# A graph layer with a segment maximum: the first sixteen gather steps of part one read stored B rows in place of x rows

## The chip, the core and the metric

The kernel runs on one core of one Trainium2 chip, in one launch. The metric is the device time of an execution in microseconds (us), stated as the median of several executions. In the tables below TensorE is called PE (its weight loads PEld), VectorE DVE, ScalarE ACT, GpSimd POOL, and the engine whose queue issues most of the transfers SP.

## The reference

The inputs are x (6250 nodes by 256 features), 100000 edges as two integer lists src and dst, sorted by dst, and two 256x256 weights with biases.

```python
x_src = x[src]
x_dst = x[dst]
theta_x = (x_dst - x_src) @ theta_w.T + theta_b
phi_x = x_src @ phi_w.T + phi_b
e = relu(theta_x + phi_x)
out = segment_max(e, dst, num_segments=6250)      # 0 for a node without edges
x = layernorm(x + out)
```

A message is x_dst @ theta + x_src @ (phi - theta) + bias. The first and the last term are the same for all edges of one node, so the maximum is needed only over B = x @ (phi - theta), at the rows that src names. The kernel computes B once for all nodes, takes maxima of rows of B by node, and adds the rest at the end.

## The kernel before, in words

**Preparation.** B is made in 13 shares of up to four tiles of 128 nodes. For each pair of tiles, PE transposes x (L779), ACT copies the result out of PSUM (L782), PE multiplies with the weights (L794), ACT copies B out (L797), and a transfer stores four tiles as rows of the DRAM tensor `b_rows` (L818). Meanwhile DVE finds where the second part's edges begin, fetches a window of 872 edges per partition (`dst_w`, `src_w`, L521), and builds a table of words from it (`fill_table`, L1005 and L1008, ten rounds).

**Part one** covers the nodes that stand first. Its edges lie as 81 steps of 128 edges. In each step one indirect transfer on POOL's queue gathers 128 rows (L528), and DVE runs a capped maximum along the steps (L699: one instruction for each step but the first). Eight steps make a group, a tile `g` of a ring of five; a finished group is stored to `maxima_1` (L714). Groups 0 and 1, which are sixteen steps, gather rows of x, because `b_rows` isn't there yet; `x_group` multiplies these rows by the weights in place, in pairs of steps, with the same four instructions as above. Groups 2 to 10 gather rows of `b_rows`. The end of part one's chain goes through PE (`tails_1`, transposes in L912).

**Part two** covers the other 44 tiles of nodes. For each of 17 slots of 383 rows of B, DVE picks which row each node wants in that slot (`choice`, L1037 to L1057, two slots at a time); `wanted` transposes the picks on PE (L1064) and stores them as `chosen_rows`; ACT and at times DVE turn them into one-hot matrices `hot` (L1121, L1123, L1126); PE multiplies the slot's rows, split into two terms (L1094 on ACT, L1095 on DVE), with them (L1134); and the maximum goes into `acc` (L1144 for slot 0, L1146 on DVE after that). What the slots leave over is written as a list (`list_pieces`, thirteen rounds on DVE, stored in L1289), fetched back by POOL in three transfers (L521), and run as 257 further steps of gather and maximum. At the end the sums are normalised and written.

**What sets the order.** Each engine works through its own instructions in order. A scheduler lays the order down when the program is built, from the order of the code and its own guesses of durations. Transfers on POOL's queue are tied to each other by `in_turn`, and L699 is tied to the gather of its step. Slot 0's L1095 stands behind `choice` of slots 8 and 9 (`ahead_of_run`). The driver at the end of the function calls `fill_table`, then `choice` and `wanted` in nine rounds, with one chunk of slot 0 after the fifth, then two more chunks, then `run_1` for groups 0 and 1, and then the rest of part one in turn with chunks and list pieces.

Of the kernel before, what the change touches and what calls it, by code (L numbers as in the profile page):

```python
# [54 lines left out]
STEPS = 8  # L55
# [1 line left out]
EARLY_SHARES = 10  # L57
RING = 5
FIRST_STEPS = 81
X_GROUPS = 2  # L60
TILES = 44
LIST = 257
WINDOW = 872
# [9 lines left out]
TABLE_BITS = 10  # L73
SLOT_BITS = 9
P_BITS = 7
EARLY_STEPS = 6
TERMS_BEHIND = 4
ROWS_AT = 2
TERMS_AT = 4
# [356 lines left out]
def gnn_kernel(ctx: ExitStack, tc: tile.TileContext, x, src, dst, theta_w, theta_b, phi_w, phi_b, out):  # L436
# [30 lines left out]
    b_rows = dram.tile([N, D], FP, name="b_rows")  # L467
# [26 lines left out]
    def present(t, part, j0, n):  # L494
        return t[: LEFT1 if (part, j0, n) == LAST else P, :n, :]
# [31 lines left out]
    def gather(to, table, offsets, wait_for=None):  # L527
        one = nc.gpsimd.indirect_dma_start(  # L528
            out=to, out_offset=None, in_=table, in_offset=bass.IndirectOffsetOnAxis(ap=offsets, axis=0)
        )  # L530
# [19 lines left out]
    src_1 = const.tile([P, T1], I32, name="src_1")  # L550
    nc.sync.dma_start(src_1, flat(src, 0, [[T1, P], [1, T1]]))
    gathered = body.enter_context(tc.tile_pool(name="gathered", bufs=RING))
    groups = [(t0, min(STEPS, T1 - t0)) for t0 in range(0, T1, STEPS)]
    of_x = range(X_GROUPS)
    ring_tiles = {}

    def gather_group(i, table, a=0, b=STEPS):
        t0, n = groups[i]
        if i not in ring_tiles:
            ring_tiles[i] = gathered.tile([P, STEPS, D], FP, name="g")  # L560
        return [
            gather(ring_tiles[i][:, k, :], table, src_1[:, t0 + k : t0 + k + 1], hold(k)) for k in range(a, min(b, n))
        ]

    first_node = const.tile([P, 1], FP, name="first_node")
# [18 lines left out]
    in_turn(iota(starts, TILES, N1 - 1 + TILES, 0))  # L584
    in_turn(iota(first_node, 0, N1, TILES))
    in_turn(iota(ids[:, T + 1 :], 0, 0, T))
    gather_group(of_x[0], x, 0, EARLY_STEPS)


    dst_1 = search.tile([P, T1 + 2], I32, name="dst_1")  # L590
    dst_i = search.tile([P, T + 2], I32, name="dst_i")
# [71 lines left out]
        windows_fetched[0] = latest[0]  # L663

    search_edges()
    gather_group(of_x[0], x, EARLY_STEPS)

    ids_1 = const.tile([P, T1 + 3], FP, name="ids_1")
    one = nc.vector.tensor_copy(ids_1[:, : T1 + 2], dst_1)
    behind_in_order(one, window_found[0], "search ahead of the first part")  # L670
    early.close()
    for i in of_x[1:]:
        gather_group(i, x)

    iota(ids_1[:, T1 + 2 :], 0, 0, T1)
    start, chunk, after = ids_1[:, T1 + 2 :], ids_1[:, 1 : T1 + 1], ids_1[:, T1 + 1 : T1 + 2]
# [50 lines left out]
    with (  # L727
# [57 lines left out]
        def b_of(to, rows, kept=None):  # L785

            n = rows.shape[1]
            x_t = x_transposed(rows)
            if kept is not None:
                nc.sync.dma_start(kept, x_t[:, :n].rearrange("p h k n -> p (h k n)"))  # L790
            ps = ps_b.tile([P, 2, D], FP, name="ps_b")
            for h in range(n):
                for k in range(KC):
                    nc.tensor.matmul(  # L794
                        ps[:, h, :], x_t[:, h, k, :], weights[:, k, 0, :], start=(k == 0), stop=(k == KC - 1)
                    )
            nc.scalar.copy(to, ps[:, :n, :])  # L797

        def x_group(i):
            for q in range(0, STEPS, 2):  # L800
                rows = ring_tiles[i][:, q : q + 2, :]
                b_of(rows, rows)

        for number, share in enumerate(shares(4)):
            if number == X_AHEAD:
                bias_and_pads()
            n = share[2]
# [8 lines left out]
                kept = x_columns[:, at : at + w * KC * P] if share[0] == 2 else None  # L816
                b_of(b_sb[:, i : i + w, :], x_q[:, i : i + w, :], kept)
            nc.scalar.dma_start(node_rows(b_rows, *share), present(b_sb, *share))  # L818
        for i in of_x:
            x_group(i)  # L820

    acc_pool = body.enter_context(tc.tile_pool(name="accs", bufs=1))
    acc = acc_pool.tile([P, KC, OWN], FP, name="acc")
# [647 lines left out]


    parts = [(s, c) for s in range(NS) for c in range(len(CHUNKS))]
    groups_1 = list(range(X_GROUPS, len(groups)))
    todo = list(range(NT1))
    searched = [None]

# [17 lines left out]
    def next_group_1(n):  # L1495
        if groups_1:
            i = groups_1.pop(0)
            if held[0]:
                g_last, (t0, n_last) = ring_tiles[i - 1], groups[i - 1]
                for k in range(0, STEPS, 2):  # L1500
                    run_steps(1, g_last, range(k, k + 2), caps_1, t0)
                    gather_group(i, b_rows, k, k + 2)
                    if k % 4 == 2 and n > k // 4:
                        fetch_parts(1)
                nc.sync.dma_start(maxima_1t[:, t0 : t0 + STEPS, :], g_last)
            else:
                gathers = gather_group(i, b_rows)
                if i > X_GROUPS:
                    run_1(i - 1, gathers)
                fetch_parts(n)  # L1510
        if searched[0] is not None:
            next(searched[0])
            searched[0] = None
        if todo:
# [12 lines left out]
    for _ in range(2):  # L1527
        next_group_1(0)
    chunk_heads()
# [127 lines left out]
```

## Time and profile before

| what | value |
|---|---|
| time, median of 3 runs | 729.33 us (724.2 to 729.99) |
| profiled execution, its own time | 723.1 us |
| span of its trace | 721.3 us |
| PE busy | 653.8 us, 91% |
| DVE busy | 634.1 us, 88% |
| ACT busy | 510.1 us, 71% |
| POOL busy | 526.9 us, 73% |

The busy shares are means over stages with different limits, so they tell little of one place. The change touches the first 230 us or so; what counts is which engine is never idle there, and which wait ends last.

### The profile page before, as it was taken

The page shows a single profiled execution, that of the slowest core. Times are in us where ns is not written, and L with a number is a line of the kernel's source. Part 1 is how long each engine was busy: PE and PEld are TensorE (multiplying, and loading weights), DVE is VectorE, ACT ScalarE, POOL GpSimd, SP SyncE. Part 2 cuts the span into 40 slices and gives each one's busy share as a digit, 9 for nine tenths or more (in the row PEclk, how much of TensorE's full clock was granted, in tenths as well). Part 3 has the DMA queues.
Part 4 walks back from the last instruction along what each step waited for, and adds up shares of the span by engine and source line. Part 5 has one row for each costly group of instructions (what it writes and reads, how often), then busy time and mean ns, then how long its engine had stood idle before and what let it go on. Part 6 is the DMA issues. An engine that isn't in the chain of part 4 may idle for free.

```text
span 721.3 us, 9888 instructions
## 1 busy us (share of the span) xinstructions
PE 653.8 (91%) x2908; PEld 532.9 (74%) x2908; DVE 634.1 (88%) x1202; ACT 510.1 (71%) x597; POOL 526.9 (73%) x730
## 2 busy tenths in 40 slices
PE   4799977769798999999999999999999999969990
PEld 3688766657576888888888888888888888848870
DVE  6999999999997788989889788988988989898876
ACT  1344759679695876868778687977868778642676
POOL 6700277888815857888888888888888888848880
PEclk9999989799999999999999999999999999999996
DMA  8898563655656647777786977887776767655865
GB/s 257 296 352 300 178 205 95 225 194 171 190 197 201 208 153 224 242 228 256 221 277 213 335 263 245 273 291 256 222 248 219 250 203 247 207 188 181 293 242 214
DMA packets 60879, 167.06 MB, mean 232 GB/s; under 512 B 11896, under 2 KB 21905, under 8 KB 54673
## 3 DMA queue, kind: packets, MB, share of 16 engines
q1 hardware_dynamic: 39717, 107.15, 42.5%
q0 software_dynamic: 18976, 52.35, 24.7%
q10 hardware_dynamic: 2124, 6.84, 2.5%
q8 instruction: 25, 0.41, 0.2%
q14 instruction: 37, 0.30, 0.1%
HBM read 102.94 MB, written 63.36 MB: 231 GB/s over the span
## 4 chain that ended last, share of the span: by engine, by line
PE 62%; DVE 17%; POOL 6%; DMA 5%; ACT 5%; issue 4%; ACTq 0%; DVEq 0%; POOLq 0%
PE ps_f L1134 60%; POOL g L528 4%; DVE g L699 3%; DVE words L1008 2%; ACT hot L1123 1%; ACT hot L1126 1%; DVE work L1005 1%; POOL pause L498 1%; ACT x_f L1434 1%; DVE wide L1041 1%; DMA g<-maxima,place 1%; DMA dst_w<-in_dst_dram,window 1%; DMA dst<-in_dst_dram 1%; DMA dst_w<-list_words,run_start 1%; DMA list_words<-work 1%
## 5 line engine op out<-in xcount | busy, mean ns | idle before, releaser
L1134 PE MATMUL ps_f<-hot,terms 128*128 128x512 f32 x2156 | 512.0, 399 | 23.3 <-ACT hot L1126 9.9
L1134 PEld LDWEIGHTS ps_f<-hot,terms 128*128 128x128 f32 x2156 | 409.6, 192 | 120.2 <-ACT hot L1126 17.0
L528 POOL DMA_INDIRECT g<-b_rows,list_src x256 | 258.0, 1008 | 58.5 <-issue 35.1
L1123 ACT ACTIVATE hot<-want,minus_row 128x1024 fp32r<-128x1024 f16 x210 | 216.4, 1078 | 100.9 <-PE ps_f L1134 100.9
L1146 DVE TENSOR_TENSOR acc<-acc,ps_f 128x1024 f32<-128x1024 f32 x192 | 215.7, 1129 | 52.2 <-PE ps_f L1134 51.3
L1126 ACT ACTIVATE hot<-hot 128x2048 fp32r<-128x2048 f32 (+2 forms) x102 | 186.6, 1829 | 2.6
L699 DVE SCALAR_TENSOR_TENSOR g<-g,caps 128x256 f32<-128x256 f32 x335 | 160.7, 480 | 1.9
L528 POOL DMA_INDIRECT g<-b_rows,src x65 | 92.1, 1418 | 69.6 <-DMA b_rows<-b_sb 49.8
L498 POOL IOTA pause<- 128x160 f32 x312 | 97.3, 312 | 2.3
L794 PE MATMUL ps_b<-weights,x_t 128*128 128x256 f32 x260 | 62.1, 394 | 7.5 <-ACT x_t L782 7.1
L1121 DVE TENSOR_SCALAR hot<-want,row_id 128x1024 fp32r<-128x1024 f16 x84 | 61.6, 734 | 0.3 <-issue 0.3
L794 PEld LDWEIGHTS ps_b<-weights,x_t 128*128 128x128 f32 x260 | 49.2, 195 | 16.0 <-ACT x_t L782 9.8
L528 POOL DMA_INDIRECT g<-maxima,place x44 | 42.6, 968 | 17.8 <-DMA maxima<-g 10.9
L1389 PE MATMUL ps_e<-weights,kept 128*128 128x256 f32 x176 | 41.6, 379 | 0.0
L1419 ACT ACTIVATE squares<-x_f,r 128x256 bf16<-128x256 f32 x49 | 24.2, 494 | 21.9 <-DVE r L1416 21.9
L1389 PEld LDWEIGHTS ps_e<-weights,kept 128*128 128x128 f32 x176 | 33.5, 190 | 4.3
L797 ACT COPY b_sb<-ps_b 128x512 f32<-128x512 f32 (+1 forms) x25 | 14.4, 577 | 30.8 <-PE ps_b L794 21.8
L1434 ACT ACTIVATE x_f<-x_f,r 128x256 f32<-128x256 f32 x41 | 21.3, 587 | 5.7 <-DVE r L1426 5.7
L782 ACT COPY x_t<-ps_xt 128x512 f32<-128x512 f32 (+1 forms) x33 | 18.2, 589 | 7.9 <-PE ps_xt L779 7.6
L1399 DVE TENSOR_TENSOR g<-g,ps_e 128x512 f32<-128x512 f32 x22 | 15.1, 687 | 8.6 <-DMA g<-maxima,place 4.7
L528 POOL DMA_INDIRECT g<-in_x_dram,src x16 | 17.9, 1116 | 5.4 <-issue 4.1
L1144 ACT COPY acc<-ps_f 128x1024 f32<-128x1024 f32 (+1 forms) x12 | 11.3, 941 | 14.6 <-PE ps_f L1134 14.6
(251 smaller groups left out, 416.1 us busy)
## 6 DMA issues: line engine op xcount, KB each, us to landing
maxima<-g SPq DMA_DIRECT2D x42, 1024.0 KB
want<-chosen_rows SPq DMA_DIRECT2D x85, 256.0 KB
x_q<-in_x_dram SPq DMA_DIRECT2D x12, 512.0 KB
b_rows<-b_sb ACTq DMA_DIRECT2D x12, 512.0 KB
x_columns<-x_t SPq DMA_DIRECT2D x22, 256.0 KB
kept<-x_columns SPq DMA_DIRECT2D x11, 512.0 KB
raw<-b_rows SPq DMA_DIRECT2D x16, 256.0 KB
g<-b_rows,list_src POOLq DMA_INDIRECT x256, 4.3
```

What stands on the lines that cost most here:

```text
L498: return nc.gpsimd.iota(t, pattern=[[step, t.shape[1]]], base=base, channel_multiplier=per_partition, allow_small_or_imprecise_dtypes=True,)
L528: one = nc.gpsimd.indirect_dma_start(out=to, out_offset=None, in_=table, in_offset=bass.IndirectOffsetOnAxis(ap=offsets, axis=0))
L699: one = nc.vector.scalar_tensor_tensor(g[:, k, :], last[part], caps[:, t : t + 1], g[:, k, :], op0=ALU.min, op1=ALU.max)
L794: nc.tensor.matmul(ps[:, h, :], x_t[:, h, k, :], weights[:, k, 0, :], start=(k == 0), stop=(k == KC - 1))
L1121: nc.vector.tensor_scalar(hot[:, b, :], want, row_id[:, b : b + 1], None, op0=ALU.is_equal)
L1123: nc.scalar.activation(hot[:, b, :], want, AF.Abs, bias=minus_row[:, b : b + 1], scale=1.0)
L1126: nc.scalar.activation(apart, apart.bitcast(FP), AF.Relu, bias=1.0, scale=-1.0)
L1134: one = nc.tensor.matmul(ps[:, w : w + 512], terms[:, part, b, h * P : (h + 1) * P], hot[:, b, w : w + 512], start=(i == 0), stop=(i == n ...
L1146: one = nc.vector.tensor_tensor(to, to, ps, op=ALU.max)
L1389: nc.tensor.matmul(a[:, i, :], x_t[:, 2 * i + c, :], weights[:, c, 1, :], start=False, stop=(i == w - 1 and c == KC - 1))
L1419: nc.scalar.activation(squares, x_f[:, k, :], AF.Square, bias=mean[:, k : k + 1], scale=1.0, accum_out=var[:, k : k + 1])
L1434: nc.scalar.activation(x_f[:, k, :], x_f[:, k, :], AF.Identity, bias=mean[:, k : k + 1], scale=inv[:, k : k + 1])
```

## The change

Groups 0 and 1 no longer gather rows of x. The six gathers at the begin, the ten after the edge window, and `x_group` go away. After `fill_table` in the code, both groups are gathered from `b_rows` like all others, and their two `run_1` calls are tied to these gathers. The number of gathers (81), of bytes that they move, and of maxima on DVE stays as it was. The constant `X_GROUPS` is renamed `FIRST_GROUPS`, and `EARLY_STEPS` is dropped.

```diff
-    of_x = range(X_GROUPS)
     ring_tiles = {}
 
-    def gather_group(i, table, a=0, b=STEPS):
+    def gather_group(i, a=0, b=STEPS):
         t0, n = groups[i]
         if i not in ring_tiles:
             ring_tiles[i] = gathered.tile([P, STEPS, D], FP, name="g")
         return [
-            gather(ring_tiles[i][:, k, :], table, src_1[:, t0 + k : t0 + k + 1], hold(k)) for k in range(a, min(b, n))
+            gather(ring_tiles[i][:, k, :], b_rows, src_1[:, t0 + k : t0 + k + 1], hold(k)) for k in range(a, min(b, n))
         ]
...
     in_turn(iota(ids[:, T + 1 :], 0, 0, T))
-    gather_group(of_x[0], x, 0, EARLY_STEPS)
...
     search_edges()
-    gather_group(of_x[0], x, EARLY_STEPS)
-
...
     early.close()
-    for i in of_x[1:]:
-        gather_group(i, x)
...
-        def x_group(i):
-            for q in range(0, STEPS, 2):
-                rows = ring_tiles[i][:, q : q + 2, :]
-                b_of(rows, rows)
-
...
             nc.scalar.dma_start(node_rows(b_rows, *share), present(b_sb, *share))
-        for i in of_x:
-            x_group(i)
...
-                gathers = gather_group(i, b_rows)
-                if i > X_GROUPS:
+                gathers = gather_group(i)
+                if i > FIRST_GROUPS:
                     run_1(i - 1, gathers)
...
     fill_table()
+    first_gathers = [gather_group(i) for i in range(FIRST_GROUPS)]
     for s0 in range(0, NS, BATCH_S):
...
     fetch_parts(2)
-    for i in of_x:
-        run_1(i)
+    for i in range(FIRST_GROUPS):
+        run_1(i, first_gathers[i])
```

The changed kernel's lines lie up to 15 lower than the same lines before. POOL, from the edge window on, before (`dst_w` and `src_w` are the window, `g` a group of part one, `pause` a filler):

```order
L521 DMA dst_w<-in_dst_dram,window 128x872
L498 IOTA pause 128x160
L521 DMA src_w<-in_src_dram,window 128x872
L498 IOTA pause 128x160
L528 DMA g<-in_x_dram,src_72 128x256 x10
L498 IOTA order 128x1584
L498 IOTA chunk_1248 128x1
L1284 IOTA owner 128x1
L498 IOTA chunk_2064 128x1
L528 DMA g<-b_rows,src_72 128x256 x24
L498 IOTA wide 128x290
L528 DMA g<-b_rows,src_72 128x256 x41
```

and of the change:

```order
L520 DMA dst_w<-in_dst_dram,window 128x872
L497 IOTA pause 128x160
L520 DMA src_w<-in_src_dram,window 128x872
L497 IOTA pause 128x160
L497 IOTA order 128x1584
L497 IOTA chunk_1144 128x1
L1269 IOTA owner 128x1
L497 IOTA chunk_1960 128x1
L527 DMA g<-b_rows,src_72 128x256 x40
L497 IOTA wide 128x290
L527 DMA g<-b_rows,src_72 128x256 x41
```

Ten gathers from x are gone here and six more near the program's begin; 40 gathers from `b_rows` stand where 24 stood.

PE, at the end of B, before (`ps_b` is B, `ps` with `chosen` are the picks of two slots, `ps_f` the slots' products; `x_q` is a tile of x, `g` a group):

```order
L1064 MATMUL ps<-ident,chosen 88x128 x2
L794 MATMUL ps_b<-weights,x_t 128x256 x12
L779 MATMUL ps_xt<-ident,g 128x128 x10
L794 MATMUL ps_b<-weights,x_t 128x256 x8
L779 MATMUL ps_xt<-ident,g 128x128 x10
L1064 MATMUL ps<-ident,chosen 88x128 x2
L794 MATMUL ps_b<-weights,x_t 128x256 x12
L779 MATMUL ps_xt<-ident,g 128x128 x4
L1064 MATMUL ps<-ident,chosen 88x128
L794 MATMUL ps_b<-weights,x_t 128x256 x4
L1064 MATMUL ps<-ident,chosen 88x128
L1134 MATMUL ps_f<-hot,terms 128x512 x26
```

and of the change:

```order
L1049 MATMUL ps<-ident,chosen 88x128 x2
L786 MATMUL ps_b<-weights,x_t 128x256 x4
L1049 MATMUL ps<-ident,chosen 88x128
L1119 MATMUL ps_f<-hot,terms 128x512 x4
L1049 MATMUL ps<-ident,chosen 88x128
L1119 MATMUL ps_f<-hot,terms 128x512 x2
L1049 MATMUL ps<-ident,chosen 88x128
L1119 MATMUL ps_f<-hot,terms 128x512 x20
```

The 32 transposes of `g` and their 32 products are gone, and the first six slot products stand between the picks; the next twenty follow the fifth round of picks.

DVE, in the fourth round of `choice` (L1037 to L1057), before:

```order
L1041 TENSOR_TENSOR wide<-wide 128x1056
L699 TENSOR_SCALAR g<-g,caps_171 128x256
L1041 TENSOR_TENSOR wide<-wide 128x2x264
L699 TENSOR_SCALAR g<-g,caps_171 128x256
L1041 TENSOR_TENSOR wide<-wide 128x2x132
L1041 TENSOR_TENSOR wide<-wide 128x2x44
L699 TENSOR_SCALAR g<-g,caps_171 128x256
L1041 TENSOR_TENSOR wide<-wide 128x2x44
L699 TENSOR_SCALAR g<-g,caps_171 128x256
L1048 TENSOR_SCALAR at<-wide 128x88
L1049 COPY chosen<-at 128x88
L1053 TENSOR_TENSOR wide<-wide,at 128x2112
```

and of the change, from that round's L1048 on (now L1033) to the first minimum of the fifth round:

```order
L1033 TENSOR_SCALAR at<-wide 128x88
L691 TENSOR_SCALAR g<-g,caps_153 128x256
L1034 COPY chosen<-at 128x88
L1038 TENSOR_TENSOR wide<-wide,at 128x2112
L691 TENSOR_SCALAR g<-g,caps_153 128x256
L1042 TENSOR_TENSOR unused<-unused,wide 128x1056
L691 TENSOR_SCALAR g<-g,caps_153 128x256
L1042 TENSOR_TENSOR unused<-unused,wide 128x1056
L1022 TENSOR_SCALAR wide<-padded 128x1056 x2
L691 TENSOR_SCALAR g<-g,caps_153 128x256
L1026 TENSOR_TENSOR wide<-wide 128x1056
L691 TENSOR_SCALAR g<-g,caps_153 128x256
```

Group 0's seven maxima (L699, now L691) began inside the third round and ended in the fourth; now the first two stand just ahead of the rows shown, around the fourth round's last 44-wide minimum, and the seventh stands inside the fifth round, ahead of four of its minima. Each of them waits for its own gather. The seven are still all ahead of slot 0's L1095. Behind the first rounds of the list the order on every engine is as before.

More of the change, by code (lines that the diff above doesn't have):

```diff
@@ L59 @@
 FIRST_STEPS = 81
-X_GROUPS = 2
+FIRST_GROUPS = 2
 TILES = 44
@@ L75 @@
 P_BITS = 7
-EARLY_STEPS = 6
 TERMS_BEHIND = 4
@@ L1473, in gnn_kernel @@
     parts = [(s, c) for s in range(NS) for c in range(len(CHUNKS))]
-    groups_1 = list(range(X_GROUPS, len(groups)))
+    groups_1 = list(range(FIRST_GROUPS, len(groups)))
     todo = list(range(NT1))
@@ L1501, in next_group_1 @@
                     run_steps(1, g_last, range(k, k + 2), caps_1, t0)
-                    gather_group(i, b_rows, k, k + 2)
+                    gather_group(i, k, k + 2)
                     if k % 4 == 2 and n > k // 4:
```

## The prediction

> **What bounds the kernel now.** The change moves work in the first 230 us, so I read the stretches of that time first, then DVE's waits in them, then the single rows around the place. The busy time of each engine by stretch (columns: window, its length, then PE, PEld, DVE, ACT and POOL busy with counts, granted PE clock, DMA share, GB/s):
>
> ```profile
> 20.00:60.00 40.00, 35.86 (x186) 30.65 (x185) 38.96 (x44) 16.65 (x31) 11.98 (x12) 0.96 0.95 330
> 60.00:101.00 41.00, 35.20 (x182) 29.58 (x180) 39.48 (x81) 27.51 (x44) 13.46 (x13) 0.97 0.66 226
> 101.00:150.00 49.00, 37.34 (x138) 29.25 (x139) 48.01 (x109) 34.86 (x43) 38.87 (x28) 0.85 0.48 162
> 150.00:222.00 72.00, 60.78 (x246) 47.28 (x246) 67.91 (x108) 62.34 (x61) 44.11 (x32) 0.95 0.61 194
> 222.00:400.00 178.00, 178.00 (x777) 145.16 (x777) 151.77 (x255) 136.70 (x115) 146.93 (x221) 0.99 0.69 221
> ```
>
> From 20 to 222 us the third engine column, DVE, has next to no gap (38.96 of 40, 48.01 of 49), while PE has 11.7 us free of 49 in one stretch. From 222 us on PE has none at all. So DVE sets the pace first and PE after it, and the handover is the thing to watch. DVE's waits from 60 to 222 us (engine and line, whom it waited for, total us, times, longest):
>
> ```profile
> DVE dst_w L1301 <- DMA dst_w<-list_words,run_start: 3.1, 1, 3.1
> DVE acc L1146 <- PE ps_f L1134: 0.6, 2, 0.3
> ```
>
> DVE waits for PE only 0.6 us, and never for a gathered row. Its one long wait is at the end of the stage, for POOL's transfer of the list. The handover in order of time:
>
> ```profile
> 196.68 1.26 POOL L528 DMA_INDIRECT g<-b_rows,src  x1 [0.30 <-DVE g L699]
> 214.09 1.14 POOL L521 DMA_INDIRECT dst_w<-list_words,run_start  x1 [16.15 <-DMA list_words<-work]
> 220.35 0.49 DVE L1301 COPY_PREDICATED dst_w<-words,dst_w 128x290 int32<-128x290 int32 x1 [3.08 <-DMA dst_w<-list_words,run_start]
> 220.73 0.48 DVE L699 SCALAR_TENSOR_TENSOR g<-g,caps 128x256 f32<-128x256 f32 x1
> 221.26 0.69 PE L912 MATMUL ps<-ident,g 128*128 128x128 f32 x2 [2.58 <-DVE g L699]
> 221.60 31.74 PE L1134 MATMUL ps_f<-hot,terms 128*128 128x512 f32 x132
> ```
>
> POOL ends its 65 gathers from B, idles 16.15 us until DVE's list is stored, and fetches it. DVE takes the fetched list (L1301), then the last maximum of part one, then PE turns it round (L912) and runs without a gap. Nothing after 222 us can take a delay back, as PE is full there. So what L912 is late by, the kernel is late by, one to one.
>
> **What is removed.** PE and ACT lose the second multiplication (groups of lines in the window 74 to 101.4 us: count, busy us, mean ns, idle before):
>
> ```profile
> L794 PE MATMUL ps_b<-weights,x_t 128*128 128x256 f32 x72 | 17.6, 402 | 2.6 <-ACT x_t L782 2.5
> L779 PE MATMUL ps_xt<-ident,g 128*128 128x128 f32 x32 | 4.1, 273 | 0.0
> L782 ACT COPY x_t<-ps_xt 128x512 f32<-128x512 f32 x9 | 4.8, 612 | 0.0
> L797 ACT COPY g<-ps_b 128x512 f32<-128x512 f32 x8 | 4.7, 586 | 5.9 <-PE ps_b L794 5.8
> ```
>
> 64 of the 72 products are of `g`: 15.6 us, with the transposes 19.7 us of PE; on ACT 8 of 9 and 8 copies, 4.3 + 4.7 = 9.0 us. I cost this **at zero**. In these 27 us DVE is the engine without a gap, it loses no instruction, and slot 0's second term (L1095) must come from it before PE can go on:
>
> ```profile
> 77.76 0.33 ACTq L818 DMA_DIRECT2D b_rows<-b_sb  x1
> 83.88 0.97 POOL L528 DMA_INDIRECT g<-b_rows,src  x1 [49.76 <-DMA b_rows<-b_sb]
> 84.53 0.70 DVE L1041 TENSOR_TENSOR wide<-wide 128x1056 int16<-128x1056 int16 x1
> 90.25 0.48 DVE L699 SCALAR_TENSOR_TENSOR g<-g,caps 128x256 f32<-128x256 f32 x1
> 92.07 1.99 DVE L1041 TENSOR_TENSOR wide<-wide 128x1056 int16<-128x1056 int16 x5
> 94.41 0.95 POOL L528 DMA_INDIRECT g<-b_rows,src  x1 [0.30 <-issue]
> 97.10 0.95 DVE L1095 TENSOR_TENSOR terms<-raw,terms 128x768 fp32r<-128x768 f32 x1
> 101.45 7.84 PE L1134 MATMUL ps_f<-hot,terms 128*128 128x512 f32 x26
> ```
>
> L1095 ends at 98.05, and PE's slots begin at 101.45 behind the last products of `g`. At most the 3.4 us between can be won on PE, and DVE, not PE, ends the stage.
>
> **What is added: a wait on DVE.** Group 0's maxima now need rows of B. `b_rows` is complete at 83.88, where POOL had waited 49.76 us for it; the eighth gather behind that starts at 94.41. DVE did its seventh maximum at 90.25, on rows that were long there. In the changed order the seventh stands in the fifth round, and it needs the eighth gather (step 7). Behind a maximum that waits there stand the round's four minima, the picks and L1095, and PE waits for L1095. How long a gather takes, from the first five of B (us, least, median, most), and over all sixteen from x, while the DMA engines were fuller:
>
> ```profile
> DMA to landing us min/median/max: 2.7/2.8/2.9
> g<-in_x_dram,src POOLq DMA_INDIRECT x16, 5.9
> ```
>
> I take 3.0, near the first, which is of the same gathers at the same time.
>
> When B is complete shifts too. The sixteen gathers from x fell into the fullest DMA stretch (share 0.95), and in it ACT waited for a store of B, and PE for ACT:
>
> ```profile
> 27.99 0.58 ACT L797 COPY b_sb<-ps_b 128x512 f32<-128x512 f32 x1 [6.36 <-DMA b_rows<-b_sb]
> 29.11 3.08 PE L794 MATMUL ps_b<-weights,x_t 128*128 128x256 f32 x8 [3.92 <-ACT x_t L782]
> 20.34 0.83 DVE L979 TENSOR_SCALAR wide<-dst_w,first_node 128x872 f32<-128x872 int32 x1 [1.59 <-DMA dst_w<-in_dst_dram,window]
> ```
>
> With ten gathers less around it, PE's 3.92 us pause shrinks; between 0 and 3.9 I take 2.5. DVE's own start can gain up to 1.59, which it then only waits longer for the rows, so it isn't counted.
>
> The sum: the eighth gather starts at 94.41 - 2.5 = 91.9, lands at 94.9; the maximum takes 0.5 (0.48 in its rows); from behind the round's first minimum (92.07 + 0.70 = 92.77) to the end of L1095 (98.05) are 5.3. L1095 ends at 94.9 + 0.5 + 5.3 = 100.7, **2.6 us later** than before. Bounds: 1.3 with all 3.9 won, 5.1 with nothing won, 8.0 with nothing won and 5.9 to land.
>
> **What is moved: sixteen gathers to the far end of POOL's queue.** All of POOL's later work, the other groups' gathers and the three list fetches, stands behind them. Do rows come too late elsewhere? The gathers of groups 2 to 10 each come sixteen places later. The tightest place before the end is the maximum of step 44: it would use the gather that the 45th of `b_rows` is now:
>
> ```profile
> 161.98 1.72 POOL L528 DMA_INDIRECT g<-b_rows,src  x1 [0.30 <-issue]
> 165.04 0.48 DVE L699 SCALAR_TENSOR_TENSOR g<-g,caps 128x256 f32<-128x256 f32 x1
> 120.09 0.39 POOL L498 IOTA wide<- 128x290 f32 x1 [1.65 <-DVE unused L1057]
> 121.16 3.69 POOL L528 DMA_INDIRECT g<-b_rows,src  x1 [0.68 <-DVE g L699]
> 120.33 3.67 DVE L1241 SCALAR_TENSOR_TENSOR work<-padded,unused 128x1584 f32<-128x1584 int16 x1
> 131.92 0.95 POOL L528 DMA_INDIRECT g<-b_rows,src  x1 [0.30 <-issue]
> 142.78 2.95 POOL L528 DMA_INDIRECT g<-b_rows,src  x1 [0.30 <-issue]
> ```
>
> It starts at 161.98, less 2.5, less 1.9 for the stop at 120 us (the waits of 1.65 and 0.68, of which some 0.4 stay as the step to the filler's new place), so at 157.6, and lands at 160.6, 4 us ahead of 165.04. That holds. The queue's end doesn't hold as surely. The 65th gather starts at 196.68 - 4.4 = 192.3 and sixteen more follow. Eight intervals from 131.92 to 142.78, beside short DVE instructions, are 1.36 each; the forty from 121.16 to 196.68 are 1.89 each, since some stretch beside long DVE instructions (3.69 beside a 3.67 one). After 197 us DVE has only short ones, so I take 1.4: the last gather starts at 214.7, and POOL is free at 215.9. The list would be there at 214.09 + 2.6 = 216.7, so the sixteen are **hidden by 0.8 us**. At 1.89 POOL is free at 223.8, or 226.3 if B comes no earlier: 9.7 to 12.2 late.
>
> The Trainium skill ("SBUF — State Buffer", SBUF: two separate sides) says that VectorE and GpSimd share a port pair under an exclusive lock, held for a whole instruction. The 3.69 us gather beside the 3.67 us instruction agrees; by that rule the sixteen, which before ran partly beside small instructions at the begin, pay for every long DVE instruction that they meet.
>
> The total is 2.6 us: 723.1 of the profiled execution become 725.7. That execution lies 6.2 under the median of the runs shown, so on the median I forecast 729.33 + 2.6 = **731.9 us**.
>
> **The rivals.**
> *POOL's queue becomes the bound (slower).* The place is the fetch at 214.09; the price is 9.7 to 12.2, giving 739.0 to 741.5. It decides as soon as the last sixteen intervals exceed (216.7 - 1.25 - 192.3) / 16 = 1.45 us. For it: the mean of 1.89. Against it: 1.36 beside short instructions.
> *The rows land slowly, or B comes no earlier (slower).* 5.9 to land and no shift: 8.0 late, 737.3. For it: DVE waits seven times in turn. Against it: 2.9 at most for the first five.
> *The hole pays (faster).* If B comes early enough for DVE not to wait, DVE keeps its earlier start, 1.6, and PE begins with L1095 at 96.5 in place of 101.45, 4.9 earlier: 724.4 if PE carries it to the end, 727.7 if DVE does. It needs rows 2.6 us earlier than forecast before DVE loses nothing, and 4.2 for the whole, while B has only 1.4 more to win. For it: 19.7 us of PE's work are gone. Against it: PE waited in the slots as it is, and a pause costs it speed:
>
> ```profile
> 136.89 8.38 PE L1134 MATMUL ps_f<-hot,terms 128*128 128x512 f32 x24 [3.88 <-ACT hot L1126]
> 161.31 5.79 PE L1134 MATMUL ps_f<-hot,terms 128*128 128x512 f32 x24 [0.98 <-ACT hot L1126]
> ```
>
> After a pause of 3.88 us the same 24 products take 2.6 us more. The changed PE has only picks and six early products in some 20 us ahead of the slots, so even this rival loses 2.6 of its 4.9 on PE. The Trainium skill ("TensorE: Matmul & The Clock Gate", What's actually happening) states that an idle window of about 3.4 us halves the clock; the rows agree, and the rule speaks against this rival.
>
> **How the numbers follow.** A measurement of this kernel can tell about 1%, 7.3 us, from no change. Chances: the forecast, 1.3 to 5.1 late, 0.55; POOL's queue 0.24; slow rows 0.09; the hole 0.12, of which 0.05 goes past 1%. So faster 0.05, within 1% 0.55 + 0.07 = 0.62, slower 0.24 + 0.09 = 0.33. The range goes down to 726, which is inside the third rival and also the forecast's low end (1.3) on the lowest run shown, 724.2; it goes up to 741, which leaves out only the top of POOL's rival.
>
> **What would show it.** Right: seven maxima of group 0 wait for gathers between 85 and 96 us; L1095 ends near 100.7; PE has some 20 us nearly free before the slots; POOL idles a little or not at all at the list fetch; L912 near 224. Wrong: POOL's last gather from `b_rows` after 220 us, then the queue has set the end; L912 before 221, then PE's and ACT's relief did reach the end; DVE waiting for gathers past 130 us, then the slack of 4 us was misjudged.

## The result, and the profile after

The changed kernel is a little **slower**: 728.52 us as the median of twenty runs (724.53 to 736.58), against 724.55 for twenty of the kernel before (722.12 to 729.99). The ratio is 1.0048, with a 95% interval from 1.0025 to 1.0071. A later comparison gave 729.5 against 726.0, ratio 1.0065 (1.0032 to 1.0097). The profiled execution has a span of 726.9 us, 5.6 more than that of before.

One thing is needed to read the experiments: in three of their five sessions, called disturbed below, every kernel ran slower, the kernel before at 746 to 749 us on chips of which two ran it in 726 us later, so every ratio is to the kernel before in its own session, and a ratio from a disturbed session is not one to build on.

Two stages of the profile after, in the windows and columns of the prediction:

```profile
60.00:101.00 41.00, 17.27 (x68) 12.16 (x66) 35.23 (x72) 17.42 (x24) 15.67 (x14) 0.71 0.51 176
222.00:400.00 178.00, 175.01 (x762) 142.38 (x762) 151.20 (x261) 136.98 (x116) 143.68 (x218) 0.99 0.69 225
```

Half of PE's work between 60 and 101 us is gone (17.27 us busy in place of 35.20), and its granted clock there fell from 0.97 to 0.71. DVE, which had 39.48 busy us in that stretch, now has 35.23: it stands still for some 4 us more. From 222 us on PE isn't full at once as it was before: 175.01 of 178, because its last stage begins later. DVE's waits from 60 to 240 us (engine and line, whom it waited for, total us, times, longest):

```profile
DVE g L691 <- DMA g<-b_rows,src: 7.4, 6, 2.1
DVE acc L1131 <- PE ps_f L1119: 1.6, 3, 1.1
DVE terms L1080 <- ACT terms L1079: 1.4, 1, 1.4
DVE dst_w L1286 <- DMA dst_w<-list_words,run_start: 0.3, 1, 0.3
```

Two of these are new: 7.4 us for gathered rows, and 1.4 us for ScalarE's half of a slot's terms. The lines of this kernel are up to 15 lower: L1080 is the subtraction that was L1095, L897 is L912. POOL, then DVE, then PE around the last round that stands ahead of the slots, each in the order of its queue:

```profile
81.37 1.43 POOL L527 DMA_INDIRECT g<-b_rows,src  x1 [63.02 <-DMA b_rows<-b_sb]
91.40 2.42 POOL L527 DMA_INDIRECT g<-b_rows,src  x1 [0.30 <-issue]
87.12 0.48 DVE L691 SCALAR_TENSOR_TENSOR g<-g,caps 128x256 f32<-128x256 f32 x1 [2.12 <-DMA g<-b_rows,src]
96.09 0.48 DVE L691 SCALAR_TENSOR_TENSOR g<-g,caps 128x256 f32<-128x256 f32 x1 [2.08 <-DMA g<-b_rows,src]
100.76 0.95 DVE L1080 TENSOR_TENSOR terms<-raw,terms 128x768 fp32r<-128x768 f32 x1
108.22 0.96 DVE L1080 TENSOR_TENSOR terms<-raw,terms 128x768 fp32r<-128x768 f32 x1 [1.36 <-ACT terms L1079]
101.77 7.73 PE L1119 MATMUL ps_f<-hot,terms 128*128 128x512 f32 x20 [3.08 <-DVE terms L1080]
```

B is complete at 81.37, 2.5 us sooner than before. The first gather is issued at once, the eighth at 91.40, and that one takes 2.42 us to issue. DVE waits 2.12 us for the first rows and 2.08 for the eighth gather's, and L1080 starts at 100.76 where L1095 started at 97.10: **3.66 us later**. The second subtraction starts at 108.22, after 1.36 us of waiting for ScalarE. PE waits for L1080, too, but takes up the slots at 101.77, only 0.32 us later than before (101.45), with six of their products already done: what is late from here on is DVE. Why ScalarE is late at the second subtraction (its rows of that time):

```profile
106.44 1.01 ACT L1129 COPY acc<-ps_f 128x1024 f32<-128x1024 f32 x1 [7.45 <-PE ps_f L1119]
107.35 0.83 ACT L1079 CAST terms<-raw 128x768 fp32r<-128x768 f32 x1
```

With PE's products gone the scheduler laid ScalarE's instructions down in another order: the cast L1079 stands behind an eviction (L1129, a copy out of PSUM) that itself waits 7.45 us for PE's products of slot 0. In the kernel before the cast stood ahead of it. The end of the stage:

```profile
194.78 1.32 POOL L527 DMA_INDIRECT g<-b_rows,src  x1 [0.30 <-DVE g L691]
218.19 0.95 POOL L527 DMA_INDIRECT g<-b_rows,src  x1 [0.30 <-DVE place_f L867]
220.50 0.94 POOL L520 DMA_INDIRECT dst_w<-list_words,run_start  x1 [1.36 <-DMA list_words<-work]
221.45 0.48 DVE L691 SCALAR_TENSOR_TENSOR g<-g,caps 128x256 f32<-128x256 f32 x1 [1.62 <-DMA g<-b_rows,src]
226.10 0.49 DVE L1286 COPY_PREDICATED dst_w<-words,dst_w 128x290 int32<-128x290 int32 x1 [0.29 <-DMA dst_w<-list_words,run_start]
227.01 0.44 PE L897 MATMUL ps<-ident,g 128*128 128x128 f32 x2 [2.98 <-DVE g L691]
227.21 32.04 PE L1119 MATMUL ps_f<-hot,terms 128*128 128x512 f32 x132
```

POOL's 65th gather from B is the row at 194.78, its 81st that at 218.19. It still waits 1.36 us for the list, so its queue isn't the bound. The last maxima do wait for rows (1.62 at 221.45), but beside the list's transfer, which ends later, by the 0.29 us that L1286 still waits. PE turns the last maximum round at 227.01, 5.75 us later than before, and runs on without a gap (the row of 132 products). The rest of the span, 499.9 us, is as long as it was (500.0).

### The profile page after: what moved, and what is told of

Read it like the earlier page. It is cut to its first block, busy times and chain, and to the rows that moved or that the text cites. A ratio compares the mean times of both kernels' runs of the same rounds, so it can differ in the third digit from the quotient of the medians.

```text
span 726.9 us, 9661 instructions
## 1 busy us (share of the span) xinstructions
PE 640.8 (88%) x2812; PEld 519.6 (71%) x2812; DVE 635.6 (87%) x1202; ACT 502.1 (69%) x581; POOL 528.6 (73%) x730
## 5 line engine op out<-in xcount | busy, mean ns | idle before, releaser
L1119 PE MATMUL ps_f<-hot,terms 128*128 128x512 f32 x2156 | 517.9, 401 | 35.0 <-DVE hot L1106 15.4
L527 POOL DMA_INDIRECT g<-b_rows,src x81 | 113.1, 1397 | 87.2 <-DMA b_rows<-b_sb 63.0
L691 DVE SCALAR_TENSOR_TENSOR g<-g,caps 128x256 f32<-128x256 f32 x335 | 160.6, 480 | 9.3 <-DMA g<-b_rows,src 7.4
L786 PE MATMUL ps_b<-weights,x_t 128*128 128x256 f32 x196 | 47.0, 393 | 1.7 <-ACT x_t L774 1.4
L786 PEld LDWEIGHTS ps_b<-weights,x_t 128*128 128x128 f32 x196 | 36.9, 194 | 8.5 <-ACT x_t L774 3.7
L1129 ACT COPY acc<-ps_f 128x1024 f32<-128x1024 f32 (+1 forms) x12 | 11.3, 940 | 17.6 <-PE ps_f L1119 17.6
L1384 DVE TENSOR_TENSOR g<-g,ps_e 128x512 f32<-128x512 f32 x22 | 15.1, 686 | 7.9 <-DMA g<-maxima,place 4.2
L774 ACT COPY x_t<-ps_xt 128x512 f32<-128x512 f32 (+1 forms) x25 | 13.9, 585 | 7.0 <-PE ps_xt L771 6.8
L1264 DVE COPY_PREDICATED work<-words,work 128x316 int32<-128x316 int32 (+9 forms) x11 | 18.3, 1661 | 0.0
```

The lines of the kernel that those rows point to most:

```text
L527: one = nc.gpsimd.indirect_dma_start(out=to, out_offset=None, in_=table, in_offset=bass.IndirectOffsetOnAxis(ap=offsets, axis=0))
L691: one = nc.vector.scalar_tensor_tensor(g[:, k, :], last[part], caps[:, t : t + 1], g[:, k, :], op0=ALU.min, op1=ALU.max)
L786: nc.tensor.matmul(ps[:, h, :], x_t[:, h, k, :], weights[:, k, 0, :], start=(k == 0), stop=(k == KC - 1))
L1119: one = nc.tensor.matmul(ps[:, w : w + 512], terms[:, part, b, h * P : (h + 1) * P], hot[:, b, w : w + 512], start=(i == 0), stop=(i == n ...
L1384: nc.vector.tensor_tensor(some, some, ps[:, :w, :], op=ALU.max)
```

## Experiments

All diffs are against the changed kernel unless they say otherwise. Where the expectations speak of slower chips, the disturbed sessions are meant: the chips themselves were not slower.

### Take the wait away: group 0's maxima behind the last choice

```diff
-                if part == 1 and k == 0 and ahead_of_run[0] is not None:
+                if part == 1 and k == (t0 == 0) and ahead_of_run[0] is not None:
                     behind_in_order(one, ahead_of_run[0], "choice and list ahead of the first part")
```

Group 0's step 0 issues no instruction, so the tie on `k == 0` never held that group back. The edit puts it on step 1: in the last trace of it the first maximum starts at 117.34 and not at 87.12, and the gathers have 30 us more to land. Gathers, queue and PE's gap stay.

> The changed kernel, with group 0's maxima tied behind the last round of choice, so DVE has no early wait while POOL keeps its sixteen more gathers. The slots' first L1095 should end at 96 to 98 instead of 101.7. Theory 'wait' alone: no loss, 0.998 to 1.002. Theory 'queue': POOL is free no earlier than about 218, 4 to 5 us behind the 214.1 of before, so the loss stays, 1.005 to 1.007. My view is both in a row: either alone is enough for some 4 us, so it stays near 1.005.

> The changed kernel with group 0's maxima put behind the last choice instead of ahead of it. If the loss of the changed kernel is VectorE's wait for the gathers at 85 to 96 us, that wait is gone and the ratio is 0.998 to 1.002; if the loss is the gap on TensorE with its lower clock, or POOL's sixteen further gathers, both of which stay, it is 1.003 to 1.007.

> e3 (group 0's maxima behind the last choice) once more, for a chip on which the changed kernel's loss is the 0.5 to 0.65% of its first comparison: 0.997 to 1.002 if the loss is the wait, and L897 in its trace by 223 us; 1.004 to 1.008 if not.

Measured: 0.9997 (0.9967 to 1.0026) where I had expected 1.005, 0.9953 (0.9918 to 0.9988), and in an undisturbed session 0.9993 (0.9972 to 1.0015). In that session's trace, DVE's first subtraction, POOL's last gather and first fetch of the list, and PE's handover:

```profile
92.97 0.95 DVE L1080 TENSOR_TENSOR terms<-raw,terms 128x768 fp32r<-128x768 f32 x1
214.52 0.95 POOL L527 DMA_INDIRECT g<-b_rows,src  x1 [0.30 <-issue]
215.77 1.11 POOL L520 DMA_INDIRECT dst_w<-list_words,run_start  x1 [0.30 <-issue]
221.31 0.44 PE L897 MATMUL ps<-ident,g 128*128 128x128 f32 x2 [3.75 <-DVE g L691]
```

L1080 is back before 97, L897 at 221.31, and the loss is gone. POOL's fetch now follows its last gather at once (0.30 of issue, no wait for the list), so the fetch has no slack left here.

The control is the same one-line edit in the kernel **before**, where group 0's rows were there at 82 us and nothing waited:

> The kernel before with the same one-line edit as e3: group 0's maxima behind the last choice. It is the control of e3. If e3 wins back only the wait that the change brought, the edit is worth nothing here, since those rows have landed by 82 us: 0.998 to 1.002. If the edit has a gain of its own, because the choice ends earlier by eight maxima of 0.48 us and TensorE starts on the slots earlier, the ratio is 0.993 to 0.997, and e3 is a loss and a gain that cancel.

> The kernel before with group 0's maxima behind the last choice, the control of e3, once more at undisturbed times. If e3 only takes back the wait that the change brought: 0.998 to 1.002. If the edit has a gain of its own, which in e3 would cancel a loss: 0.993 to 0.997.

Measured: 1.0004 (0.9972 to 1.0037) and 1.0038 (1.0014 to 1.0063), both in disturbed sessions, so the control is weaker than e3 itself. Neither shows a gain of the edit's own behind which e3 could hide a loss. The undisturbed trace of e3 shows none either: seven maxima went behind the first subtraction, which starts 2 to 4 us earlier than in the kernel before, but the list is stored no earlier (207.98, against 208.90 and 207.45).

### Lengthen the wait at unchanged work

```diff
-    first_gathers = [gather_group(i) for i in range(FIRST_GROUPS)]
+    first_gathers = [gather_group(i) for i in (1, 0)][::-1]
```

> The changed kernel with its first sixteen gathers issued in the other order, group 1's eight ahead of group 0's, so that group 0's rows land eight gathers, some 10 to 11 us, later; all else is the same work. If the loss is VectorE's wait ahead of the last choice, the wait grows by that much and so does the loss: 1.016 to 1.022 of the kernel before. If the loss has another cause (the longer queue, the work gone from TensorE), the order of the gathers changes nothing: 1.004 to 1.008.

Measured: **1.0133** (1.0099 to 1.0167), 735.5 us. More than the changed kernel, less than I expected. DVE's first and sixth maximum of group 0, its subtraction, and PE's handover:

```profile
95.40 0.48 DVE L691 SCALAR_TENSOR_TENSOR g<-g,caps 128x256 f32<-128x256 f32 x1 [6.54 <-DMA g<-b_rows,src]
101.59 0.49 DVE L691 SCALAR_TENSOR_TENSOR g<-g,caps 128x256 f32<-128x256 f32 x1 [0.65 <-DMA g<-b_rows,src]
105.03 0.95 DVE L1080 TENSOR_TENSOR terms<-raw,terms 128x768 fp32r<-128x768 f32 x1
232.65 0.69 PE L897 MATMUL ps<-ident,g 128*128 128x128 f32 x2 [4.86 <-DVE g L691]
```

The first rows come 8.1 us later than in the changed kernel (95.40 against 87.30 in the trace of a3, below), but L1080 only 4.0 later (105.03 against 101.02): while it waited in small pieces DVE did the rest of the choice in between, which I had left out. The list is stored 3.7 us later than in a3. L897 is 5.9 us later and the span 5.3, since from its store to the handover the list took 2.2 us longer; why, the trace doesn't show. The order of the gathers alone changes the time, with no instruction added (the scheduler laid all seven maxima into the fifth round, behind more of the choice than in the changed kernel). So some 4 us of the added loss come from when the rows land, and the other 2 are open.

### Give PE and ScalarE their work back, or take it away alone

```diff
             nc.scalar.dma_start(node_rows(b_rows, *share), present(b_sb, *share))
+        warm = prep.tile([P, 2, D], FP, name="warm")
+        for _ in range(8):
+            b_of(warm, w_in[:, 0])
```

The second kernel (e5) is the kernel before without its `for i in of_x: x_group(i)`; it leaves out the second multiplication, and group 0's maxima, which wait for no product then, stand earlier on DVE. For both, the changed kernel and the kernel before were traced in the same session.

> The changed kernel once more, as the measure for the next two on this chip. Expected from 1.0048 on the first chip and 1.0184 on another: 1.004 to 1.019.

> The kernel before, unaltered, for a trace of it on the chips on which the variants ran: there it takes 746 to 749 us and not 724.6. If the time that these chips add is ScalarE and TensorE standing still at 105 to 125 us for something that no row names, as in the traces of the variants, it is in this trace too, with 5 us or more of such waits between 95 and 150 us; if the variants bring those waits themselves, this trace has under 1 us of them.

> The changed kernel with sixteen products of a tile of weights put in where the kernel before multiplied groups 0 and 1: TensorE and ScalarE get the 19.7 and 9.0 us of work back, in their old places, for nothing; the gathers, their queue and VectorE's wait for them stay those of the changed kernel. If the loss is VectorE's wait, it stays: a ratio as that of the changed kernel on this chip, at least 1.003. If the loss is the gap on TensorE (its clock fell to 0.5 at 80 to 110 us) or the new order of ScalarE's instructions that comes with it, it goes: 0.998 to 1.002.

> The kernel before without the products of groups 0 and 1, so that the first part's maxima run over rows of x there (this leaves out the second multiplication with the weights). No wait for gathers, no longer queue on POOL, but TensorE has the gap of the changed kernel. If the gap costs nothing, 0.996 to 1.002; if the gap costs what the changed kernel lost, 1.003 or more.

Measured: the changed kernel 1.0065 (1.0032 to 1.0097); with the products back (e10) **1.006** (1.0034 to 1.0087), the same; the kernel before without them (e5) **1.0001** (0.9978 to 1.0025). The kernel before took 724.44 in its traced run, so its trace could not show what the 746 to 749 us contain. Its trace, then that of the changed kernel (a3), each with the first subtraction and the handover:

```profile
94.94 0.95 DVE L1095 TENSOR_TENSOR terms<-raw,terms 128x768 fp32r<-128x768 f32 x1
222.12 0.69 PE L912 MATMUL ps<-ident,g 128*128 128x128 f32 x2 [4.90 <-DVE g L699]
```

```profile
101.02 0.95 DVE L1080 TENSOR_TENSOR terms<-raw,terms 128x768 fp32r<-128x768 f32 x1
226.77 0.44 PE L897 MATMUL ps<-ident,g 128*128 128x128 f32 x2 [2.72 <-DVE g L691]
```

And e10: the stretch from 60 to 101 us, group 0's first and seventh maximum, both subtractions, PE's start on the slots, the handover:

```profile
60.00:101.00 41.00, 32.93 (x167) 28.10 (x166) 33.65 (x69) 25.83 (x41) 15.43 (x13) 0.94 0.56 186
86.84 0.48 DVE L691 SCALAR_TENSOR_TENSOR g<-g,caps 128x256 f32<-128x256 f32 x1 [2.70 <-DMA g<-b_rows,src]
96.94 0.52 DVE L691 SCALAR_TENSOR_TENSOR g<-g,caps 128x256 f32<-128x256 f32 x1 [2.54 <-DMA g<-b_rows,src]
101.64 0.95 DVE L1083 TENSOR_TENSOR terms<-raw,terms 128x768 fp32r<-128x768 f32 x1
109.09 0.95 DVE L1083 TENSOR_TENSOR terms<-raw,terms 128x768 fp32r<-128x768 f32 x1
105.99 7.89 PE L1122 MATMUL ps_f<-hot,terms 128*128 128x512 f32 x26
226.97 0.69 PE L900 MATMUL ps<-ident,g 128*128 128x128 f32 x2 [3.89 <-DVE g L691]
```

PE is busy for 32.93 us at a granted clock of 0.94, nearly as before, and the wait for ScalarE at the second subtraction is gone (109.09 has none), since its order is that of before again. The waits for rows are there (2.70, 2.54), and L900, which is L897 here, is as late as in the changed kernel. PE takes up the slots 4.2 us later than in the trace after (105.99 against 101.77), yet the list is stored 1.0 us earlier (213.26 against 214.22): the delay doesn't reach the end through PE's start. In e5 it's the other way round:

```profile
60.00:101.00 41.00, 25.12 (x106) 19.27 (x105) 39.20 (x76) 20.07 (x28) 12.80 (x13) 0.76 0.64 206
95.66 0.95 DVE L1093 TENSOR_TENSOR terms<-raw,terms 128x768 fp32r<-128x768 f32 x1
221.68 0.69 PE L910 MATMUL ps<-ident,g 128*128 128x128 f32 x2 [3.36 <-DVE g L699]
```

PE has the gap of the changed kernel (25.12 us, of which some 4 are slots that begin inside the window; clock 0.76), no row is late ahead of the slots, and nothing is lost that can be told. So neither the 19.7 us of PE nor its colder clock nor ScalarE's order makes the loss by itself.

### Lengthen POOL's queue alone

The kernel before, with gathers of groups 2 and on put at the front of POOL's queue, whose rows are gathered again at their old place:

```diff
     fill_table()
+    for i in (2, 3):            # (2, 3, 4) in e15
+        gather_group(i, b_rows)
```

> The kernel before, with groups 2 and 3 gathered twice, which puts sixteen gathers more ahead of the others on POOL's queue and changes nothing for DVE, PE and ACT. Theory 'queue': POOL is free near 219 instead of 198, the list fetch starts 5 us later than 214.1, ratio 1.005 to 1.008. Theory 'wait': 0.998 to 1.002.

> The kernel before with sixteen further gathers at the head of POOL's queue, once more: its first comparison (1.0003) was made while the kernel before itself took 746 us and not 726. With 24 further gathers the ratio was 1.0172, POOL's last gather ended at 227.0 us and the list's fetch followed it at once. Eight gathers fewer end 10 to 11 us earlier, at 216 to 217, some 3 us behind the list's arrival in the kernel before (213 to 214): by that 1.003 to 1.005. If the queue is hidden, as the forecast held for the changed kernel, 0.998 to 1.002.

> The kernel before with 24 further gathers of b_rows at the head of POOL's queue, where e4 had 16 and cost nothing (1.0003). If the queue of the forecast holds, 16 gathers end about 1 us ahead of the list's arrival and each further one makes the list's fetch about 1.35 us later: 8 of them 9 to 11 us, less the 1 us of slack, so 1.011 to 1.014. If POOL's queue does not carry the list's fetch on the path, 1.000 to 1.003.

Measured: sixteen more 1.0003 (0.9967 to 1.004) and 1.0018 (0.9981 to 1.0054), both in disturbed sessions; twenty-four more, in an undisturbed one, **1.0172** (1.013 to 1.0215), above the 1.011 to 1.014 expected. With sixteen (e4_again), POOL's last gather and the fetch of the list:

```profile
218.80 0.95 POOL L528 DMA_INDIRECT g<-b_rows,src  x1 [0.30 <-issue]
220.05 0.95 POOL L521 DMA_INDIRECT dst_w<-list_words,run_start  x1 [0.30 <-issue]
```

The fetch comes straight behind the gathers; the list, stored from 212.43 and some 5 to 6 us under way, was there 1 to 2 us earlier. With twenty-four, DVE's wait for rows, POOL, DVE's taking of the list, and PE:

```profile
DVE g L699 <- DMA g<-b_rows,src: 14.4, 11, 3.3
226.05 0.95 POOL L528 DMA_INDIRECT g<-b_rows,src  x1 [0.30 <-issue]
227.30 0.94 POOL L521 DMA_INDIRECT dst_w<-list_words,run_start  x1 [0.30 <-issue]
232.36 0.48 DVE L1301 COPY_PREDICATED dst_w<-words,dst_w 128x290 int32<-128x290 int32 x1
233.27 0.69 PE L912 MATMUL ps<-ident,g 128*128 128x128 f32 x2 [3.88 <-DVE g L699]
```

The fetch is late, and DVE waits 14.4 us, eleven times, for rows that stand behind the copies; nine of these waits, 10.3 us, come before the list, which is stored at 219.68. DVE then takes the list at 232.36 without waiting for it, so in this trace it is the late rows that set the end, and the late fetch, which alone I had counted, is hidden beside them. With sixteen gathers more the fetch has no slack left, with twenty-four the queue costs 1.7%: the forecast's 0.8 us of cover was as narrow as that.

### Half the change

Group 0 from x with its products as before and group 1 from `b_rows` (e1), or the other way round (e2).

```diff
+    gather_group(0, x, 0, 6)         # and gather_group(0, x, 6) behind search_edges()
...
+        x_group(0)
...
-    first_gathers = [gather_group(i) for i in range(FIRST_GROUPS)]
+    first_gathers = {1: gather_group(1, b_rows)}
```

> Group 0 gathers x as before (and is multiplied once more), group 1 gathers B: DVE's early maxima wait for nothing, and POOL's queue is eight gathers longer at its end instead of sixteen. Theory 'wait' (DVE's wait for group 0's rows makes the loss): no loss, ratio 0.998 to 1.002. Theory 'queue' (the longer queue makes it): POOL is free eight gathers of 1.4 us, 11 us, earlier than in the change's trace (219.1), so at 208, before the list is stored: no loss either. If both are wrong, it stays near 1.005.

> The other way round: group 0 gathers B, group 1 gathers x. DVE waits as in the change, and POOL has eight more gathers at its end as in the run with group 0 from x. Theory 'wait': the whole loss, ratio 1.004 to 1.007, L1095's counterpart ends 3 to 4 us later than before. Theory 'queue': none, 0.998 to 1.002.

> The changed kernel once more, unaltered, beside the kernel before, so that the next runs are compared with it on one and the same chip. Expected from its first comparison (1.0048, from 1.0025 to 1.0071): a ratio between 1.002 and 1.008. In its trace the first subtraction of the slots (L1080) again ends about 3.5 us later than in the kernel before, where the trace is of the same chip.

> Group 0 from x, group 1 from b_rows, the same kernel as e1_first_from_x, which measured 1.0132 where 0.998 to 1.002 was expected. In that trace ScalarE and TensorE show waits that no engine or transfer ends (11.6 us of TensorE at L1127, 9.3 us of ScalarE at L1137), which the traces of the kernel before and after do not have at all. If these belong to that chip and not to the kernel, another chip shows none of them and the ratio is 0.998 to 1.004; if the kernel itself makes them, the ratio is again 1.009 to 1.017.

> e1 (group 0 from x and multiplied as before, group 1 from b_rows) once more. It lost 1.3 and 1.45% on two slower chips without any wait for gathers. By the wait theory it is 0.998 to 1.003 on a chip whose traces have none of the idle stretches of ScalarE between 105 and 125 us; 1.009 or more again would mean that half the change costs more than the whole, for a reason that the theory lacks.

Measured: e1 1.0132 (1.0095 to 1.0169) and 1.0145 (1.0101 to 1.0189) in disturbed sessions, but **1.0015** (0.9992 to 1.0038) in an undisturbed one. e2 was 1.0062 (1.0029 to 1.0095), and the changed kernel itself 1.0184 (1.0128 to 1.0241), where I had expected at most 1.008; both are from disturbed sessions, and the second rests on two executions. In the traces of e1's two misses stand waits that the undisturbed one doesn't have. ScalarE's waits from 95 to 130 us in e1_again, and what became of it on DVE:

```profile
ACT acc L1137 <- issue: 7.2, 1, 7.2
ACT acc L1137 <- remote: 6.7, 1, 6.7
ACT rows L1059 <- issue: 5.9, 1, 5.9
DVE capped L893 <- PE ps L892: 10.6, 1, 10.6
```

Of ScalarE's three waits that the profile puts down to no row, the first has its like in the undisturbed trace, a wait for PE's products of slot 0. The other two, 6.7 and 5.9 us, have none, and no undisturbed trace has such a row on ScalarE; their cause stays open. PE then waits for ScalarE, and DVE 10.6 us for PE. In the undisturbed trace ScalarE waits for PE's products alone, and DVE's first subtraction stands where the kernel before has it (94.94 to 97.10):

```profile
ACT acc L1137 <- PE ps_f L1127: 9.1, 3, 7.5
96.49 0.95 DVE L1088 TENSOR_TENSOR terms<-raw,terms 128x768 fp32r<-128x768 f32 x1
```

By the wait theory group 0 is the half that costs, and e1, which keeps it on x, costs nothing that can be measured, though its traced execution hands over 3 us late (225.03, in the table below). e2, the half with the wait, was run only in a disturbed session, where its 1.0062 carries no weight of its own. Its trace shows the wait, though: its first subtraction starts at 104.61, 19.4 us behind POOL's first gather from B (85.24), which is the distance in both undisturbed traces of the changed kernel, while the three traces of e1 have it at 96.3 to 96.5.

### The traces side by side

Starts of rows in the undisturbed traces, us: DVE's first subtraction, SP's store of the list, PE's handover (L912 or its heir), then the span and the difference of the two.

| trace | subtraction | list stored | handover | span | span less handover |
|---|---|---|---|---|---|
| before, first and second | 97.10, 94.94 | 208.90, 207.45 | 221.26, 222.12 | 721.3, 722.6 | 500.0, 500.5 |
| after, first and second (a3) | 100.76, 101.02 | 214.22, 214.28 | 227.01, 226.77 | 726.9, 727.6 | 499.9, 500.8 |
| e10, products back | 101.64 | 213.26 | 226.97 | 727.4 | 500.4 |
| e13, wait lengthened | 105.03 | 218.00 | 232.65 | 732.9 | 500.2 |
| e3, wait away | 92.97 | 207.98 | 221.31 | 722.9 | 501.6 |
| e1, group 0 from x | 96.49 | 209.90 | 225.03 | 725.6 | 500.6 |
| e5, no products | 95.66 | 208.54 | 221.68 | 721.9 | 500.2 |
| e15, queue of 24 more | 95.46 | 219.68 | 233.27 | 734.4 | 501.1 |

From the list's store to the handover 12.4 to 15.1 us go by, and two traces of the same kernel before differ there by 2.3 (12.4 and 14.7). A handover read from one trace is no surer than that.

## Why the prediction was wrong, step by step

The mechanism was right, the size of its main term was short, and it was wrong to forecast no difference that can be told.

**What bounds the kernel**: held. The span behind the handover is 499.9 to 501.6 us in all ten traces; what the handover is late by, the kernel is late by.

**What is removed, costed at zero**: held as far as the times can tell. Putting 19.7 us of PE's work back (e10) or taking it away alone (e5) moves nothing. It was not free of consequences, though: it moved ScalarE's cast behind an eviction, 1.36 us of wait at the second subtraction, which the sum didn't have. That wait is on DVE's path: from the first subtraction to the list's store the table has 111.6 to 112.5 us in the three traces without it (before twice, e10) and 112.9 to 113.5 in four that have it in full (after twice, e1, e5). e5 and e1 have it and lose nothing that can be told, and e10 loses as much without it, so its share of the loss, at most some 1.4 us, isn't measured apart.

**When B is complete**: forecast 2.5 us sooner, measured 83.88 - 81.37 = 2.51 in the first pair of traces, but 82.84 - 81.69 = 1.15 in the second. That the first agreed so closely was in part luck.

**The added wait on DVE: the term that failed.** I forecast the first subtraction 2.6 us late, with bounds of 1.3 and 8.0. It was late by 3.66 in the first pair of traces and 101.02 - 94.94 = 6.1 in the second. Two things were off. The eighth gather started at 91.40, near the 91.9 forecast, but took 2.42 us to issue and not 0.95, and its rows came at 96.1, not 94.9: 1.2 us. I had put the row with 2.41, which stood at the sixth gather in the trace of before, into the spacing only. And the place that I measured from isn't fixed. In the kernel before DVE runs free there, and L1095 starts at 97.10 in one trace and 94.94 in the other; in the changed kernel it is pinned to POOL, and L1080 starts at 100.76 and 101.02, 19.4 and 19.3 us behind the first gather from B. A difference to one trace of the free engine was 2 us too small for the other. That seven maxima would wait in turn was too many: three of the seven did, for 4.5 us, since the rows came at intervals that the choice's own instructions filled.

**From there to the handover**: the list's store is 5.3 and 6.8 us later in the two pairs, the handover 5.75 and 4.65, the medians 4.0 and 3.5. The forecast carried 2.6 through unchanged; in the first pair ScalarE's 1.36 came on top. The path is DVE's: PE's wait for L1095, which I had named beside it, isn't what carries the delay, as PE's start on the slots in after (0.32 us late) and in e10 (4.2 us later still, with the list no later) shows.

**The moved gathers, hidden by 0.8 us**: held, by luck in part. POOL's 65th gather started at 194.78 where I had 192.3, sixteen more took (218.19 - 194.78) / 16 = 1.46 us each where I had 1.4, and POOL was free at 219.1, 3.2 later than forecast. The list came 3.8 later than forecast, too, so 1.36 us of cover remained. By my own rule (above 1.45 the queue decides) it would have been the bound, had DVE been only 2.6 us late; in e3 and e4, where DVE isn't late, the fetch comes straight behind the gathers. The slack of 4 us for later rows held until 221 us. What I had not priced is the last maxima themselves: they wait 2.96 us for their rows, and only because the list ended 0.29 us later did that cost nothing.

**The rivals**: POOL's queue set nothing here, by those 0.29 us (1.40 in a3); e15 gives its price, 1.0172 for eight gathers more than the tie, and there it works through late rows. The hole paid nothing (e10, e5). The eighth gather's rows came 4.7 us after its start and not 3.0, and 1.5 us of that is its longer issue.

**The numbers**: the median of three runs, 729.33, lay 4.8 above that of twenty, 724.55, so 731.9 was 3.4 above the measured 728.52 while the change itself was 1.4 short. And I had taken 1% as what a measurement can tell. Twenty runs against twenty tell a quarter of that, so that a forecast of 2.6 us late was a forecast of slower, and most of my chance on "within 1%" was put on a difference that can be seen.

No variant beats the kernel before: e3, the best of them, is as fast (0.9993), not faster.

## What to carry to other kernels

Work taken from an engine that isn't the bound was worth nothing here, even 20 us of it, while waits of 4.5 us put on the engine that is the bound cost 3.5 to 4.0 us of the time; so ask of each operand that now comes later which queue its reader stands in, and what stands behind that reader. Where the wait can't be avoided, move the reader: one tie in the program's order took the whole loss back here. And a wait pins a free-running engine to its supplier, so measure the delay from more than one trace of the free engine.

## What was not expected of the hardware

A gather's issue on POOL is mostly 0.95 us, but a few are far longer, and not only beside a long instruction of DVE. The longest in the trace after, with the longest DVE row beside it:

```profile
152.00 11.31 POOL L527 DMA_INDIRECT g<-b_rows,src  x1 [0.30 <-issue]
159.91 2.01 DVE L1264 COPY_PREDICATED work<-words,work 128x1580 int32<-128x1580 int32 x1
```

The gather took 11.31 us, though no DVE instruction in that time took more than 2.01. The Trainium skill ("SBUF — State Buffer", SBUF: two separate sides) says that the loser of the port shared by VectorE and GpSimd is blocked until the holder's instruction ends. A single such hold can't make 11.31 us here; several in a row might, but what held the gather isn't in the trace. It comes again: the undisturbed trace of e1 has a gather of 11.31 us at 147.78, while those of before and e3 have no gather from B above 4.5 us up to 220 us.
